# A graph layer with a guarded fast path: the guard taken from bounds ahead of the last tiles, and its branch placed in front of the last two scatters

## The chip, the cores and the metric

The kernel runs on one core of a Trainium2 chip. The time is device time in microseconds (us), the median of several executions. One further execution was recorded by the hardware profiler; its span runs from the first to the last instruction of the program.

## The reference

One layer of a graph transformer on 3125 nodes with 256 features each, and 53125 weighted edges sorted by their target. It adds three things to its input `x`:

```python
xn = _layernorm(x)
x = x + gnn(xn, edges) + mix(xn)          # graph convolutions; linear attention
x = x + ffn(_layernorm(x))                # mixture of 8 experts, one per token
# inside ffn
pos = (cumsum(one_hot, axis=0) * one_hot).sum(-1) - 1
kept = pos < C                            # C = 489 slots for each expert
hmid = relu(einsum('ecd,edf->ecf', buf, w1) + b1[:, None, :])     # 256 -> 1024
ybuf = einsum('ecf,efd->ecd', hmid, w2) + b2[:, None, :]          # 1024 -> 256
y = nan_to_num(ybuf[idx, min(pos, C - 1)] * (prb * kept)[:, None], posinf=1e4, neginf=-1e4)
```

The graph part multiplies sparse sums of edges (`segment_sum`) with two small weights, each followed by a softmax. `nan_to_num` is what the guard of this case is about: where every expert's output is finite, it changes nothing.

## The kernel before

**Two versions of one layer.** `network(runs)` is traced twice. `network(True)` relies on things that the inputs may or may not satisfy: edges sorted by target so that every group of five nodes has its edges in one run of 128 (`from_runs`), certain counts of tokens for each expert, and finite outputs, so that `nan_to_num` can be left out. While it runs it gathers a verdict: `held["found"]` (all edges were found), `full` and `low` (the counts), and `row_sums`, one sum for each token and tile of the experts' outputs (`OUTER` = 24 tiles). At its end all are multiplied into one number, `right`. Then every engine loads `right` into a register and meets a branch: with `right` = 0 the whole layer is computed again by `network(False)`, which makes no assumption; otherwise it is jumped over.

**Stages of `network(True)`.** First, `from_runs` builds the dense 3125 x 3125 adjacency matrix in 40 batches of 16 groups (`batch`, L627: matmuls of two selection matrices, copied by ACT, written to DRAM by two DMAs of the SP queue, L649 and L650). Beside that, rows of it are read back (`load_rows`, L652, tiles `a` in the pool `first_a`): strip 0 in tiles tagged `a0`, and the first rows of strip 1 in tiles tagged `a1`, some of them asked for ahead of the last batches (L715). All of this stage has a hand-written order on every engine (`tc.manual_schedule()`), and the queue of SP takes writes and reads in that order. The tiles are consumed in the order in which they were asked for (`take`, L675). Then three passes of dense products over all strips follow (L272, tiles `at`), with the attention and the gating beside them.

**The experts.** Tokens are scattered into `xbuf`, with slots for each expert. The experts' slots are worked through in halves of up to 256 slots. For each half: `turned` (L1113) normalizes the rows (DVE, tile `xs` in the pool `normed`, two buffers), transposes them on TensorE and copies them with ACT; `inner` (L1132) makes 8 blocks of hidden units with Relu on ACT; `outer` (L1148) multiplies them with w2, in tiles of 128 slots, adds the weighted bias (`bx`, L1162) and the residual (`y`, L1174, both DVE, from the pool `fin`), and scatters the rows into `out` with an indirect DMA of POOL (L1192). `chain` interleaves the halves: transposes of a half, then the second matmuls of the half before, then its own first matmuls. `outer` is a generator that yields after half of a tile's matmuls and between tiles. In this stage TensorE's order is written by hand; the order of the other engines is found by a planner, which simulates the program and puts an instruction where its engine would otherwise be idle.

**The end.** The last half has 233 slots, one tile of 128 and one of 105. Behind its last `y` stand the check of the row sums (L1521, L1522), a matmul that adds up over the partitions (L1527), `right_i` (L1529), the register loads (L1537), the branch (L1538) and the program's closing instructions (L1585). On the path that jumps over `network(False)`, each engine raises its semaphores by what the skipped code would have raised; POOL does it for the queues of its own DMAs with one instruction (INC_SWDGE_SEM), after waiting until they have landed.

Of the kernel before, what the change touches and what calls it, by code (L numbers as in the profile page):

```python
# [62 lines left out]

EPS = 1e-5
FMAX = 3.4028234663852886e38


def rows_all(ap, offset, n):
# [5 lines left out]
def gps_layer(ctx: ExitStack, tc: tile.TileContext, a: dict, out: bass.AP):  # L74
# [202 lines left out]
    def load_constants():  # L277
# [61 lines left out]

        return finish()  # L340

    def network(runs):

        with ExitStack() as net:
            layer(net, runs)

    def layer(net, runs):
# [67 lines left out]
        def from_runs():  # L415
# [136 lines left out]
            pre = ph.enter_context(tc.tile_pool(name="pre", bufs=2))  # L552
            wide = ph.enter_context(tc.tile_pool(name="wide", bufs=2))
            stage = ph.enter_context(tc.tile_pool(name="stage", bufs=3))
            first_a = ph.enter_context(tc.tile_pool(name="first_a", bufs=4))
            ps_0 = [acc(0) for _ in range(2)]
            some, made = {}, {}
            last = NG // GB
# [91 lines left out]
                nc.sync.dma_start(rows[112:GP], st[112:GP, :ng, :])  # L650

            def load_rows(s, c, tag):  # L652
                at = first_a.tile([P, SW], FP, tag=tag, name=tag)
                k = P if c < NT - 1 else LAST
                c0 = STRIPS[s][0] * P
                nc.sync.dma_start(at[:k], adj_rows[c * P : c * P + k, c0 : c0 + SW])
                return at
# [22 lines left out]
            for b in range(last + 1):  # L680
                c = (min(NG, (b + 5) * GB) - 1) // GC
                turned = c not in turned_c
                s, step = (b - NORM_AT) // NORM, (b - NORM_AT) % NORM
                normed = 0 <= s < len(STRIPS)
                if turned:
                    turn_ends(c, *fetched[c])
                if normed and step == 0:
                    norm_a(s)
                if normed and step == 1:
                    norm_b(s)  # L690
                if normed and step == 3:
                    norm_c(s)
                if b in (22, 23):
                    next(finish, None)
                if b == 24:
                    load_w_kv()
                if b < last:
                    prepare(b + 1)
                batch(b)
                if normed and step == 3:  # L700
                    norm_d(s)
                if turned:
                    q, _ = fetched[c]
                    turn_some(c, q, edge_h, 1, 2)
                    turn_some(c, q, edge, 0, 3)
                    count(c, q)
                    if c > 1 and c + 2 < NC:
                        fetched.append(gather(c + 2))
                if b in (4, 6):
                    search(1 + b // 2)  # L710
                if b == 4:
                    fetched.append(gather(3))
                while (todo[0][1] + 1) * P <= (b - 1) * GB * GR:
                    ask()
                if last - 6 < b <= last - 2:  # L715
                    ask(more, ready_1, "a1")
                while len(ready) > 2 and b > NORM_AT + 1:
                    take()
# [293 lines left out]
        net.callback(mm_pools.remove, mm_pools[-1])  # L1012
        wts_0 = net.enter_context(tc.tile_pool(name="wts_0", bufs=EARLY, side="right"))
        xe_0 = net.enter_context(tc.tile_pool(name="xe_0", bufs=EARLY, side="right"))
        fin = net.enter_context(tc.tile_pool(name="fin", bufs=4, side="right"))
        hm_0 = net.enter_context(tc.tile_pool(name="hm_0", bufs=EARLY, side="right"))
        xeT_0 = net.enter_context(tc.tile_pool(name="xeT_0", bufs=1, side="right"))
        normed = net.enter_context(tc.tile_pool(name="normed", bufs=2, side="right"))
# [38 lines left out]
        def early_experts():  # L1057
# [42 lines left out]
                    early[r] = [early[r], xe, HALF, space_0]  # L1100
            return early, num, row, full, low

        if runs:
            tiles_done = iter(range(OUTER))
            row_sums = ranked.tile([P, OUTER], FP, name="row_sums")
            nc.vector.memset(row_sums, 0.0)
        else:
            lim = ranked.tile([P, 3], FP, name="lim")
            nc.vector.memset(lim[:, 0:1], 1e4)
            nc.vector.memset(lim[:, 1:2], -1e4)  # L1110
            nc.vector.memset(lim[:, 2:3], 0.0)
# [18 lines left out]
            nc.scalar.copy(xeT[:, :, :slots], pt.rearrange("p (d s) -> p d s", d=2)[:, :, :slots])  # L1130

        def inner(xeT, hm, w1, b1_e, slots):  # L1132
            for f in range(FC):
                p = acc(f)
                for d in range(2):
                    nc.tensor.matmul(  # L1136
                        p[:, :slots], w1[:, d, f * P : (f + 1) * P], xeT[:, d, :slots],
                        start=(d == 0), stop=(d == 1),
                    )
                nc.scalar.activation(  # L1140
                    hm[:, f, :slots], p[:, :slots], AF.Relu, bias=b1_e[:, f : f + 1], scale=1.0
                )

        def apart(group, ins):
            tc.declare_no_dep(ins.ins, group=group, reason="tokens have rows of their own")
            tc.add_to_no_dep_group(group, ins.ins)

        def outer(hm, xe, w2, b2_e, slots, group):  # L1148

            for j, c in enumerate(range(0, slots, P)):  # L1150
                n = min(P, slots - c)
                p = mm()
                for f in range(FC):
# [4 lines left out]
                    if f == FC // 2 - 1:  # L1158
# [7 lines left out]
                            if group == "early":  # L1166
                                tc.keep_in_program_order(weighted_bias)
                        yield
                y = fin.tile([P, D], FP, tag="y", name="y")[:n]
                if runs:  # L1170


                    k = next(tiles_done)
                    nc.vector.scalar_tensor_tensor(  # L1174
                        y, p[:n, :D], xe[:n, j, D + 2 : D + 3], bx, op0=ALU.mult, op1=ALU.add,
                        accum_out=row_sums[:n, k : k + 1],
                    )
                else:

                    nc.vector.tensor_tensor(y, p[:n, :D], b2_e[:n], ALU.add)  # L1180
                    nc.scalar.activation(y, y, AF.Copy, scale=xe[:n, j, D + 2 : D + 3])
                    for i in range(3):
                        mk = masks.tile([P, D], I32, tag="mk", name="mk")[:n]
                        if i == 0:
                            nc.vector.tensor_scalar(mk, y, FMAX, None, op0=ALU.is_gt)
                        elif i == 1:
                            nc.vector.tensor_scalar(mk, y, -FMAX, None, op0=ALU.is_lt)
                        else:
                            nc.vector.tensor_tensor(mk, y, y, ALU.not_equal)
                        nc.vector.copy_predicated(y, mk, lim[:n, i : i + 1].to_broadcast([n, D]))  # L1190
                    nc.vector.tensor_tensor(y, y, xe[:n, j, :D], ALU.add)
                sc = nc.gpsimd.indirect_dma_start(  # L1192
                    out=out,
                    out_offset=bass.IndirectOffsetOnAxis(
                        ap=xe[:n, j, D + 3 : D + 4].bitcast(I32), axis=0
                    ),
                    in_=y,
                    in_offset=None,
                    bounds_check=N - 1,
                    oob_is_err=False,  # L1200
                )
                apart(group, sc)
                if c + P < slots:
                    yield

# [6 lines left out]
        def chain(group, halves):  # L1212

            for (w1, w2, b1_e, b2_e), xe, slots, space in halves:
                xeT, hm = space()
                turned(xe, slots, xeT, group == "early")
                yield
                if front:
                    yield from outer(*front.pop())
                inner(xeT, hm, w1, b1_e, slots)  # L1220
                front.append((hm, xe, w2, b2_e, slots, group))
                yield

        def space_0():
# [160 lines left out]
        with tc.manual_schedule(engines={mybir.EngineType.PE}):  # L1385
# [115 lines left out]
            def work():  # L1501
                for i, (r, skip, n) in enumerate(todo):
# [5 lines left out]
                    for q, skip_q, _ in todo[i : i + 2 if runs else i + 1]:  # L1508
                        if q not in have:
                            have[q] = weights(q)  # L1510
                    yield have[r], rows_of.pop(i), n, space

            with tc.issue_after(gate_ins.ins):
                for _ in chain("out", work()):
                    pass
                outer_end(*front.pop())
            if runs:

                finite = ranked.tile([P, OUTER], FP, name="finite")
                n_finite = ranked.tile([P, 1], FP, name="n_finite")  # L1520
                nc.vector.tensor_scalar(finite, row_sums, -FMAX, None, op0=ALU.is_ge)  # L1521
                nc.vector.scalar_tensor_tensor(  # L1522
                    finite, row_sums, FMAX, finite, op0=ALU.is_le, op1=ALU.mult,
                    accum_out=n_finite,
                )
                total = mm()
                nc.tensor.matmul(total[:1, :1], ones[:, 0:1], n_finite, start=True, stop=True)  # L1527
                held["right"] = keep.tile([1, 1], I32, tag="right", name="right_i")
                nc.vector.scalar_tensor_tensor(  # L1529
                    held["right"], total[:1, :1], P * OUTER - 0.5, right, op0=ALU.is_ge,  # L1530
                    op1=ALU.mult,
                )

    network(True)


    right_v = nc.values_load(held["right"][0:1, 0:1], min_val=0, max_val=1)  # L1537
    with tc.If(right_v < 1, preferred_fallthrough_block=False):  # L1538
        network(False)


# [47 lines left out]
```

## Time and profile before

| | |
|---|---|
| median of 3 executions | 1028.1 us (1026.73 to 1030.35) |
| profiled execution | 1029.22 us |
| its span | 1027.6 us |
| granted clock of TensorE, mean over the span | 0.981 |
| busy: TensorE, DVE, ACT, POOL | 984.9, 514.0, 296.9, 92.0 us |

Engines are called PE (TensorE, matmuls), PEld (its weight loads), DVE (VectorE), ACT (ScalarE), POOL (GpSimd) and SP (SyncE, which here only issues DMAs); a `q` behind a name stands for the engine's sequencer, which waits, branches and issues. L1192 is line 1192 of the kernel. A row of instructions gives the engine, the operation, what it writes and reads, how many there were, their time, and in brackets the idle time before with what ended it. In the list of one source line the three durations are the shortest, the median and the longest in nanoseconds, and the two times behind are those of the first and the last start. In the chain of waits each row is start, length, and who held the chain. In the table by stretch the columns are the stretch, its length, then busy time and instructions of PE, PEld, DVE, ACT and POOL, the granted clock, the share of the DMA engines and GB/s.

### The profile page before, as it was taken

The numbers are of one execution on the slowest core, as the hardware profiler recorded it, in microseconds if no ns is written. First come the engines' busy times: TensorE is split into PE (matmuls) and PEld (weight loads), VectorE is DVE, ScalarE is ACT, GpSimd is POOL, SyncE is SP. The second block draws the span as 40 slices with busy tenths as digits, with TensorE's granted clock in tenths as the row PEclk, the third lists the DMA queues.
The fourth block names the chain that finished last, engine by engine and source line by source line (L and its number), as shares of the span: only waits on it lengthen the run. The fifth ranks groups of instructions, "written<-read, shape, count | busy, mean of one in ns | idle before, by whom it ended". The sixth has DMA issues, their size and how long they took to land.

```text
span 1027.6 us, 11418 instructions
## 1 busy us (share of the span) xinstructions
PE 984.9 (96%) x4198; PEld 642.5 (63%) x4198; DVE 514.0 (50%) x1144; ACT 296.9 (29%) x541; POOL 92.0 (9%) x103
## 2 busy tenths in 40 slices
PE   4999999979999999999999999999999989999995
PEld 3878888854444444455675554474444568898884
DVE  7989799800234434444653675584344454322110
ACT  2879989830001000101101001110111214222231
POOL 6301000000000000000000000000021232111111
PEclk8999999989999999999999999999999999999998
DMA  4979888983844237521375658669899886613300
GB/s 121 271 207 255 247 238 234 257 240 107 274 151 151 97 103 220 150 72 55 97 258 199 212 198 274 222 201 376 309 299 299 259 287 227 226 40 118 122 18 15
DMA packets 173104, 197.95 MB, mean 193 GB/s; under 512 B 8758, under 2 KB 119894, under 8 KB 173037
## 3 DMA queue, kind: packets, MB, share of 16 engines
q1 hardware_dynamic: 165997, 179.02, 55.8%
q0 software_dynamic: 6912, 18.10, 5.7%
q8 instruction: 35, 0.57, 0.2%
q14 instruction: 32, 0.26, 0.1%
q10 hardware_dynamic: 128, 0.00, 0.0%
HBM read 144.43 MB, written 53.37 MB: 192 GB/s over the span
## 4 chain that ended last, share of the span: by engine, by line
PE 82%; DVE 4%; DMA 3%; ACT 2%; issue 1%; SPq 1%; POOL 0%; POOLq 0%; ACTq 0%; DVEq 0%
PE acc L272 48%; PE mm L1154 7%; PE acc L1136 6%; PE acc L636 5%; PE b L636 5%; PE mm L813 4%; PE mm L869 2%; DMA at<-adj 2%; PE pk L841 1%; PE mm L896 1%; PE mm L993 1%; ACT rhs L621 1%; DMA xbuf<-rows,s_idx 1%; ACT st_rows L640 1%; PE mm L1255 0%
## 5 line engine op out<-in xcount | busy, mean ns | idle before, releaser
L272 PE MATMUL acc<-at,xn 128*128 128x512 f32 (+3 forms) x540 | 203.2, 523 | 0.9 <-DMA at<-adj 0.9
L272 PEld LDWEIGHTS acc<-at,xn 128*128 128x128 f32 (+1 forms) x540 | 96.5, 190 | 88.9 <-issue 75.3
L272 PE MATMUL acc<-at,late 128*128 128x512 f32 (+4 forms) x350 | 139.3, 549 | 3.2 <-DMA at<-adj 3.2
L272 PE MATMUL acc<-at,g 128*128 128x512 f32 (+4 forms) x350 | 137.8, 541 | 0.0
L272 PEld LDWEIGHTS acc<-at,late 128*128 128x128 f32 (+1 forms) x350 | 64.1, 195 | 63.1 <-issue 54.3
L272 PEld LDWEIGHTS acc<-at,g 128*128 128x128 f32 (+1 forms) x350 | 62.9, 190 | 58.6 <-issue 52.3
L636 PE MATMUL acc<-rhs,lhs 128*125 128x128 f32 x626 | 87.5, 284 | 8.4 <-ACT rhs L621 5.5
L636 PEld LDWEIGHTS acc<-rhs,lhs 128*125 128x125 f32 x626 | 79.3, 195 | 19.4 <-issue 7.9
L608 DVE TENSOR_TENSOR lhs<-in_row,in_blk 128x1000 f32<-128x1000 f32 (+1 forms) x79 | 90.2, 1183 | 1.6 <-DVE in_row L585 0.5
L636 PE MATMUL b<-rhs,lhs 128*125 128x128 f32 x624 | 83.4, 278 | 0.0
L272 PE MATMUL acc<-a,xn 128*128 128x512 f32 (+1 forms) x160 | 76.4, 620 | 5.2 <-DMA a<-adj 5.2
L636 PEld LDWEIGHTS b<-rhs,lhs 128*125 128x125 f32 x624 | 77.0, 194 | 0.0
L621 ACT CAST rhs<-cells 128x2048 f32<-128x2048 bf16 x39 | 74.8, 1919 | 1.2 <-DVE cells L599 1.2
L826 ACT ACTIVATE sq<-kv 128x512 f32<-128x512 f32 x25 | 15.7, 630 | 179.3 <-DVE kv L822 179.3
L1154 PE MATMUL mm<-w,hm 128*128 128x256 f32 (+2 forms) x288 | 64.3, 380 | 0.0
L819 DVE TENSOR_REDUCE kmean<-mm 128x8 f32<-128x512 f32 x25 | 17.3, 691 | 91.6 <-PE mm L813 91.6
L1136 PE MATMUL acc<-xeT,w 128*128 128x208 f32 (+2 forms) x288 | 58.1, 360 | 0.7 <-ACT xeT L1130 0.7
L1154 PEld LDWEIGHTS mm<-w,hm 128*128 128x128 f32 (+2 forms) x288 | 51.2, 180 | 9.6
L1136 PEld LDWEIGHTS acc<-xeT,w 128*128 128x128 f32 x288 | 53.3, 190 | 4.4 <-ACT xeT L1130 0.9
L640 ACT COPY st_rows<-acc 125x512 f32<-125x512 f32 (+1 forms) x79 | 47.7, 604 | 23.7 <-issue 15.1
L272 PEld LDWEIGHTS acc<-a,xn 128*128 128x128 f32 (+1 forms) x160 | 29.9, 199 | 36.7 <-issue 29.5
L1140 ACT ACTIVATE hm<-acc,b_e 128x256 f32<-128x256 f32 (+2 forms) x72 | 32.6, 455 | 69.0 <-PE acc L1136 68.9
(242 smaller groups left out, 1039.0 us busy)
## 6 DMA issues: line engine op xcount, KB each, us to landing
at<-adj SPq DMA_DIRECT2D x52, 1280.0 KB
adj<-st_rows SPq DMA_DIRECT2D x39, 896.0 KB
at<-adj SPq DMA_DIRECT2D x14, 1024.0 KB
at<-adj SPq DMA_DIRECT2D x12, 960.0 KB
w<-in_f_w SPq DMA_DIRECT2D x10, 1024.0 KB
a<-adj SPq DMA_DIRECT2D x39, 256.0 KB
at<-adj SPq DMA_DIRECT2D x12, 452.5 KB
adj<-st_rows SPq DMA_DIRECT2D x39, 104.0 KB
```

The source lines that it names most:

```text
L272: nc.tensor.matmul(ps[d][:, :w], stationary(c, d)[:k], a_rows[:k, :w], start=(c == 0), stop=(c == NT - 1),)
L608: nc.vector.tensor_tensor(lhs[:, j::k], in_row[:, j::k, :, None].to_broadcast([P, m, GR, CA]), in_blk[:, :, None, :, j].to_broadcast([P, m ...
L621: nc.scalar.copy(rhs.rearrange("p (i j) c -> p i j c", j=2), cells.rearrange("p i c j -> p i j c"),)
L636: nc.tensor.matmul(p[:GP, j * P : (j + 1) * P], lhs[:, j0 + j], rhs[:, j0 + j], start=True, stop=True,)
L640: nc.scalar.copy(st[:GP, j0 : j0 + nj, :], p[:GP, : nj * P].rearrange("p (g b) -> p g b", b=P),)
L813: nc.tensor.matmul(pkv, xnT[:, d, t * P : (t + 1) * P], w_kv[:, d, :], start=(d == 0), stop=(d == 1),)
L819: nc.vector.tensor_reduce(mean, p3, AX.X, ALU.add)
L826: nc.scalar.activation(sq, kv, AF.Square, scale=0.125)
L869: nc.tensor.matmul(p[:, j * D : (j + 1) * D], xnT[:, d, (t0 + j) * P : (t0 + j + 1) * P], w_mix[:, d, :], start=(d == 0), stop=(d == 1),)
L1136: nc.tensor.matmul(p[:, :slots], w1[:, d, f * P : (f + 1) * P], xeT[:, d, :slots], start=(d == 0), stop=(d == 1),)
L1140: nc.scalar.activation(hm[:, f, :slots], p[:, :slots], AF.Relu, bias=b1_e[:, f : f + 1], scale=1.0)
L1154: nc.tensor.matmul(p[:n, :D], hm[:, f, c : c + n], w2[:, f, :], start=(f == 0), stop=(f == FC - 1),)
```

## The change

The verdict is made earlier, from bounds instead of the last outputs:

- For the last half, Relu on ACT also gives the sums of the hidden units (`accum_out`, 8 columns of `bounds`), and five new Square activations (`squares`) give the sums of squares of this expert's w2 and b2 (5 columns). If all of these are at most 1e15, the last two tiles can't overflow. The outputs of the squares are thrown away; their tiles are taken from the buffers of `xs`.
- After half of the last half's first tile, DVE checks the 22 row sums so far and the 13 bounds, two small matmuls add them up, and DVE makes `right` and `right_i`. The register loads (`load_right`) stand ahead of the last `y`.
- After the first tile, a further matmul (`each`) spreads `right` over the partitions; DVE adds `FAR` to the tokens of the last two tiles where `right` is 0, so that their scatters fall outside of `out` and are dropped.
- The last half's outputs go into a tile of their own (`y_end`), and its two scatters are issued after the branch and after the jumped-over code. POOL and DVE have a hand-written order in this last stretch.
- For the room, `first_a` has three buffers for `a1` instead of four, with one load fewer ahead of the last batches, and `fin` has three buffers instead of four.

```diff
-            first_a = ph.enter_context(tc.tile_pool(name="first_a", bufs=4))
+            first_a = ph.enter_context(tc.tile_pool(name="first_a", bufs=1))
...
-                at = first_a.tile([P, SW], FP, tag=tag, name=tag)
+                at = first_a.tile([P, SW], FP, tag=tag, name=tag, bufs=4 if tag == "a0" else 3)
...
-                if last - 6 < b <= last - 2:
+                if last - 5 < b <= last - 2:
                     ask(more, ready_1, "a1")
...
-        fin = net.enter_context(tc.tile_pool(name="fin", bufs=4, side="right"))
+        fin = net.enter_context(tc.tile_pool(name="fin", bufs=3, side="right"))
...
         def inner(xeT, hm, w1, b1_e, slots):
+            sums = {}
             for f in range(FC):
+                if final:
+                    sums = {"accum_out": bounds[:, f : f + 1]}
...
                 nc.scalar.activation(
-                    hm[:, f, :slots], p[:, :slots], AF.Relu, bias=b1_e[:, f : f + 1], scale=1.0
+                    hm[:, f, :slots], p[:, :slots], AF.Relu, bias=b1_e[:, f : f + 1], scale=1.0,
+                    **sums,
+                )
+
+        def squares(w2, b2_e):
+            for i in range(FC // 2 + 1):
+                of = w2[:, 2 * i : 2 * i + 2, :] if i < FC // 2 else b2_e
+                junk = normed.tile([P, 2, D], FP, tag="xs", name="squares")
+                nc.scalar.activation(
+                    junk if i < FC // 2 else junk[:, 0, :], of, AF.Square,
+                    accum_out=bounds[:, FC + i : FC + i + 1],
                 )
...
+                if ends and c + P >= slots:
+                    final["load"]()
+                y = y_end[:n, j, :] if ends else fin.tile([P, D], FP, tag="y", name="y")[:n]
+                if ends:
+                    nc.vector.scalar_tensor_tensor(
+                        y, p[:n, :D], xe[:n, j, D + 2 : D + 3], bx, op0=ALU.mult, op1=ALU.add
+                    )
+                elif runs:
...
+                if not ends:
+                    apart(group, to_rows(y, xe[:n, j, D + 3 : D + 4].bitcast(I32)))
...
+                    if i == len(todo) - 1 and runs:
+                        squares(have[r][1], have[r][3])
+                        final.update(load=load_right, xe=rows_of[i])
                     yield have[r], rows_of.pop(i), n, space
...
-                outer_end(*front.pop())
...
+                ending = outer(*front.pop())
+                final_tiles = P, CAP - HALF - P
+                if runs:
+                    next(ending)
+                    n_sums = OUTER - 2
...
+                    n_bounds = bounds.shape[1]
+                    nc.vector.scalar_tensor_tensor(
+                        finite[:, :n_bounds], bounds, BOUND, ones[:, :n_bounds], op0=ALU.is_le,
+                        op1=ALU.mult, accum_out=n_finite[:, 1:2],
+                    )
+                    total = mm()
+                    for i in range(2):
+                        nc.tensor.matmul(
+                            total[:1, :1], ones[:, 0:1], n_finite[:, i : i + 1], start=(i == 0),
+                            stop=(i == 1),
+                        )
...
+                    nc.vector.tensor_copy(right_i, right)
+                with tc.manual_schedule(engines={mybir.EngineType.Pool, mybir.EngineType.DVE}):
+                    if runs:
+                        next(ending)
+                        each = mm()
+                        nc.tensor.matmul(each[:, :1], ones[0:1, :], right, start=True, stop=True)
+                        far = ranked.tile([P, 1], FP, name="far")
+                        nc.vector.tensor_scalar(
+                            far, each[:, :1], 0.5, float(FAR), op0=ALU.is_lt, op1=ALU.mult
+                        )
...
+                    for _ in ending:
+                        pass
...
-    right_v = nc.values_load(held["right"][0:1, 0:1], min_val=0, max_val=1)
-    with tc.If(right_v < 1, preferred_fallthrough_block=False):
+    with tc.If(held["right"] < 1, preferred_fallthrough_block=False):
         network(False)
+    for scatter in held["ends"]:
+        scatter()
```

## The prediction

> **What bounds the kernel now.** I read the page first (engine shares, then the chain that ended last).
>
> ```profile
> PE 984.9 (96%) x4198; PEld 642.5 (63%) x4198; DVE 514.0 (50%) x1144; ACT 296.9 (29%) x541; POOL 92.0 (9%) x103
> PE 82%; DVE 4%; DMA 3%; ACT 2%; issue 1%; SPq 1%; POOL 0%; POOLq 0%; ACTq 0%; DVEq 0%
> ```
>
> TensorE is the chain nearly everywhere, so work on DVE, ACT or POOL costs nothing unless it makes PE wait or lies behind the last matmul. Next, the chain of waits over the last stretch, and the instructions of L1538 (the branch) and L1585 (the program's end).
>
> ```profile
> 1008.07 6.92 PE mm L1154 x32
> 1014.99 0.03 issue
> 1015.01 0.50 DVE y L1174 x2
> ...
> 1015.80 0.99 POOL out L1192
> ```
> ```profile
> L1538 POOLq EVENT_SEMAPHORE  x5: 17/43/43, 1016.9 to 1017.2; - x5
> L1538 POOLq COMPARE_BRANCH  x2: 41/44/48, 1016.8 to 1019.5; - x2
> ...
> L1538 POOLq INC_SWDGE_SEM  x1: 1192/1192/1192, 1018.3 to 1018.3; - x1
> ```
> ```profile
> L1585 POOLq EVENT_SEMAPHORE  x4: 17/17/17, 1026.8 to 1027.5; - x4
> L1585 POOLq DRAIN  x3: 46/109/4219, 1022.5 to 1027.3; - x3
> ```
>
> The chain stops at the last scatter, yet the span ends at 1027.6, 12.6 us after the last matmul. Those 12.6 us are POOL's queue: y and the check until the register loads at 1016.4 (L1537); comparison and waits, 0.8; the increment (1.19), which starts only at 1018.3, when the last scatter (issued 1015.8, median landing 2.5) has landed; the jump at 1019.5, whose target starts at 1022.5, so 3.0; a drain of 4.2; closing semaphores, 0.8. The others jump earlier and are ready earlier: ACT drains at 1019.6, DVE 1020.4, PE 1021.3, SP 1023.4. POOL sets the end.
>
> A second place matters, because the diff takes one early load away. The chain of waits from 200 on, and the busy time by stretch:
>
> ```profile
> 217.81 1.03 SPq L656
> ...
> 219.36 2.79 SPq L650
> ...
> 222.25 4.00 DMA a<-adj
> ...
> 226.29 33.27 PE acc L272 x72
> ```
> ```profile
> 215.00:220.00 5.00, 2.27 (x10) 1.12 (x8) 0.00 (x0) 0.94 (x3) 0.00 (x0) 0.99 0.99 289
> 220.00:225.00 5.00, 3.78 (x4) 1.18 (x4) 0.00 (x0) 0.00 (x0) 0.00 (x0) 0.50 0.98 282
> 225.00:230.00 5.00, 3.71 (x5) 1.65 (x6) 0.18 (x1) 0.00 (x0) 0.00 (x0) 0.50 0.47 146
> ```
>
> PE waits 3.7 and 1.6 us for the rows `a`, while the DMA engines are 98 to 99% busy: there bytes set the time. The last three columns are TensorE's granted clock, the DMA share and GB/s: after the wait the clock is 0.50.
>
> **The change, part by part.** The sum is made on the profiled execution, 1029.22 us with a span of 1027.6, so 1.6 lie around it; the median of the runs is 1028.1, 1.1 lower, and I carry the difference over to it.
>
> *The tail.* The check now needs the last half's relu sums, the squares and 22 row sums. PE's part of it stands after half of the first tile: 1008.07 + 6.92/4 = 1009.8. The last relu starts at 1008.10 (0.46), its accumulator read takes 0.19 (L1270's row), the DVE check of the bounds 0.3 (L1522: 0.18 + 0.08): ready at 1009.1 to 1009.4. From that matmul to the loads it was 1016.0 to 1016.4; with a second matmul (0.16) and one more DVE copy (0.14, as L1529) 0.7: loads at 1010.5. POOL has nothing in flight then (its last scatter before the branch was issued at 1002.58), so its queue runs 0.8 + 1.2 + 3.0 without a wait: at the jump's target at 1015.6. There the two scatters stand, 1.28 apart (L1360's spacing) and 0.98 long, 2.3 together. The second y is ready at 1015.5 plus what PE got: three small matmuls now stand inside its work, at most 0.19 each (L1527, both records), 0.3 to 0.6; with 0.4 y is there at 1015.9, hidden for the second scatter. If both have to wait for DVE's count after its branch, they start at 1016.0. They end at 1017.9 to 1018.3; I take 1018.1. The drain, 4.2: 1022.3; closing 0.8: 1023.1 against 1027.6, **−4.5**; I take −4.4, for a register move or two. What is late next: PE's jump, 3.9 us (L1538), from about 1016 ends at 1020; SP's closing waits took 2.6 (1020.8 to 1023.4) and, with the second scatter landed at 1017.1 + 2.5 = 1019.6, end by 1022.2. Both stay just inside the drain.
>
> *The new waits.* On PE, `total` waits for DVE's check, with one and a half tiles queued behind it: ready 1009.4, reached 1009.8, so 0, and 0.4 us of margin. `each` waits for DVE's `right` (1010.4) and is reached after the first tile, at 1011.5: 0. On DVE `far`, two index additions (0.2 each, as the small L1521) and a register load (0.55, L1537) stand ahead of the last y, in the 3 us in which DVE idles now (1012.0 to 1015.0): 0. On POOL the load waits for `right_i`; behind it only the branch and the two scatters are queued. The first scatter goes 3.3 us later than now (1012.33), and only the end waits for it.
>
> *ACT's squares.* Four of 128x512 and one of half that, 0.63 (L826) + 0.19 each: 3.9 us. w2 of this expert was loaded long before. Their outputs take turns in the two `xs` buffers, and the last half's xs comes after them, so its norm (now at 968.32, needed at PE's transposes at 994.4) waits for the fourth. ACT's timeline has the place:
>
> ```profile
> 981.96 0.51 ACT L1130 COPY xeT<-mm 128x416 f32<-128x416 f32 x1
> 989.88 0.81 ACT L1140 ACTIVATE hm<-acc,b_e 128x208 f32<-128x208 f32 x2 [7.42 <-PE acc L1136]
> ```
>
> 7.4 us idle, from when the buffer is free (transposes at 981.9): done by 986.4, norm by 987, 7 us early. Cost 0, covered by that idle time; the third rival prices its loss. A table load isn't in the sum: after the one at L136 Relu, Copy, Exp and Tanh run without one, and Square ran beside Sqrt; Square after Exp is not shown. Two loads at L136's 1.28 make 6.5 us, still inside 7.4: 0. The Trainium skill (ScalarE: Activation LUTs, What ACT_TABLE_LOAD costs) gives about 2.66 us per switch with its drain; by an estimate from that page, 3.9 + 5.3 = 9.2 us would overrun the gap by 1.8. The relu reads add 0.19 to 0.46 in a period of 0.79: 0.
>
> *One early load fewer.* A tile of 128 x 512 floats is 262 KB; at 285 GB/s (rows above) 0.9 us. The rows PE waits for land up to 0.9 earlier; half of that is lost, since the clock is 0.50 until 230 and PE fills the time at half speed. Afterwards five tiles of lead (1.72 each, 8.6 us) stand against landings of 4.0, so no new wait. From 0 to −0.9; I take **−0.5**, the bytes' row at half clock. DMA is only 50% busy later, so the shifted load is free.
>
> *Fewer `fin` buffers.* Three y buffers at 3.5 us a tile are 10 us, against 0.8 + 2.5 until a scatter has landed: 0. y and bx of the last half: one accumulator read less each, 0.08, hidden. Buffers decide when the planner lets bx run ahead, so DVE's order may shift in the experts' stage; PE is busy there 10.0 of every 10 us from 960 to 1010, and DVE at most 2.0: 0.
>
> Sum: −4.4 − 0.5 = −4.9: span 1022.7, profiled 1024.3, median **1023.2**.
>
> **The rivals.**
> 1. *The drain starts its work when the last scatter has landed.* The trace shows it only with nothing in flight. Second scatter at 1017.1 + 2.5 = 1019.6, + 4.2 + 0.8 = 1024.6: −3.0, with the load −3.5: 1024.6. For it: a drain has something to wait for now. Against: 4.2 us of it ran 4.2 us after everything had landed, so it isn't mainly a wait.
> 2. *No gain: the end stays tied.* Either the drain ends a fixed time after the last scatter (1015.8 to 1026.7, 10.9 us; 1017.1 + 10.9 + 0.8 = 1028.8, +1.2), or the change doesn't do what it says, and POOL's branch is held until the last y (1016.0 + 0.8 + 1.2 + 3.0 + 2.3 + 4.2 + 0.8 = 1028.3, +0.7). With the load 1028.3 to 1028.8. Against the first: POOL does nothing recorded from 1019.5 to 1022.5; against the second: in the present trace each engine branches 0.4 to 0.8 after its own load, without a common wait.
> 3. *Slower: the squares stand behind the previous half's relus.* Place: ACT after 994.9. Four squares, 3.3, end at 998.2, the norm at 999.1; the transposes, which stand ahead of a whole half's matmuls in PE's fixed order, start 4.7 late. After such a wait (3.7 above) the clock was 0.50 for 10 us; over the 6.9 us of the next matmuls that loses about 3.4. +8.1 − 4.9 = +3.2: 1031.3. It decides once the fourth square ends after 993.6, a norm ahead of 994.4. Against it: DVE's order is not the program's; the last half's bx ran at 989.38, ahead of y at 998.36, which is written before it, so the planner fills idle time:
>
> ```profile
> 989.38 0.48 DVE L1162 SCALAR_TENSOR_TENSOR bx<-b_e,xe 105x256 f32<-105x256 f32 x1
> ...
> 998.36 0.48 DVE L1174 SCALAR_TENSOR_TENSOR y<-mm,xe,bx 128x256 f32<-128x256 f32 x1 [8.49 <-PE mm L1154]
> ```
>
> The Trainium skill (TensorE: Matmul & The Clock Gate, What's actually happening) lets the array return after some 3.4 us of work, an estimated 1.7 lost instead of 3.4 and a net of about +1.5; the row, with a second wait inside, shows 10 us.
>
> **How the numbers follow.** Forecast 0.52, rival 1 0.14, rival 2 0.19, rival 3 0.15. About 0.3% (3.1 us) can be told from no change in this kernel. Faster by more: the forecast and most of rival 1, 0.64; within: 0.22, rival 2 and the rest of rival 1; slower: 0.14. Low end: the load at −0.9, scatters not waiting for DVE (−0.2) and 1.0 for the drain, whose size the trace has only once: 1021.6; high end takes in rival 2: 1029.0. What is left out is rival 3 and a little below.
>
> **What would show it.** Right: POOL's jump near 1012.5, scatters at 1015.6 to 1016 and 1.3 later, a drain of 4.2 beginning near 1018, span near 1022.7; squares on ACT between 968 and 989 and PE unbroken from 960 on; the wait for `a` near 217 about 0.9 shorter. Wrong: a drain of 5 us or more (rivals 1, 2), PE idle ahead of L1126 (rival 3), POOL's branch after the last y.

## The result, and the profile after

| | before | after |
|---|---|---|
| median of the runs compared | 1028.4 us (6 runs, 1026.7 to 1030.4) | 1023.4 us (6 runs, 1020.5 to 1025.4) |
| ratio, 95% interval | | 0.9950 (0.9931 to 0.9968) |
| profiled execution, its span | 1029.2, 1027.6 us | 1024.3, 1022.7 us |

Faster by 5.1 us (0.5%), of which the interval allows 3.3 to 7.1. The prediction was 1023.2, with a span of 1022.7. That the span agrees to the tenth is partly luck, as the experiments show.

The page of the changed kernel, its engine shares and its chain that ended last:

```profile
span 1022.7 us, 11450 instructions
...
PE 983.0 (96%) x4202; PEld 640.3 (63%) x4202; DVE 514.4 (50%) x1148; ACT 300.6 (29%) x559; POOL 89.4 (9%) x103
...
POOLq 0%; POOL 0%; issue 0%
POOLq L1664 0%; POOL out L1169 0%
```

PE still works 96% of the span. The chain that ended last is now 2.3 us long (1015.33 to 1017.65) and lies wholly on POOL: it breaks off just ahead of the first of the two scatters, and no matmul is part of it any more. The rows of the branch (L1615), the register load (L1546) and the program's end (L1664), and POOL's timeline:

```profile
L1615 POOLq EVENT_SEMAPHORE  x5: 17/43/43, 1009.7 to 1010.1; - x5
L1615 POOLq COMPARE_BRANCH  x2: 41/44/48, 1009.6 to 1011.3; - x2
...
L1615 PEldq COMPARE_BRANCH  x2: 95/1862/3630, 1011.6 to 1014.9; - x2
...
L1615 POOLq INC_SWDGE_SEM  x1: 1152/1152/1152, 1010.1 to 1010.1; - x1
```
```profile
L1546 POOLq TENSOR_LOAD <-right_i x1: 297/297/297, 1009.3 to 1009.3; - x1
```
```profile
L1664 POOLq EVENT_SEMAPHORE  x4: 17/17/17, 1021.9 to 1022.6; - x4
L1664 POOLq DRAIN  x3: 46/115/6066, 1015.8 to 1022.4; - x3
```
```profile
1015.39 0.98 POOL L1169 DMA_INDIRECT out<-y_end,to_end  x1 [12.98 <-DVEq L1615]
1016.68 0.98 POOL L1169 DMA_INDIRECT out<-y_end,to_end  x1 [0.30 <-issue]
```

Read them as one queue. The load is at 1009.3 (1016.4 before). The increment begins at 1010.1, right behind the waits: no scatter is in flight that it would have to wait for, where before it started 1.0 us after the last wait, at 1018.27, just behind the landing of the last scatter that the trace records at 1018.25. The jump is issued at 1011.3 and its target starts at 1013.9. The scatters are at 1015.39 and 1016.68, 1.28 apart. The long drain is recorded from 1015.8, while the scatters still run; it ends at 1021.8, 4.17 after the second scatter's end (1017.66). The increment, the jump and its landing place are now all done while PE still multiplies; before, they came after it. DVE's timeline has the work that had to be ready:

```profile
1007.59 0.17 DVE L1570 SCALAR_TENSOR_TENSOR finite<-bounds,ones 128x13 f32<-128x13 f32 x1 [5.88 <-ACT hm L1150]
...
1009.09 0.14 DVE L1585 CAST right_i<-right 1x1 int32<-1x1 f32 x1
...
1014.77 0.48 DVE L1204 SCALAR_TENSOR_TENSOR y_end<-mm,xe,bx 105x256 f32<-105x256 f32 x1 [2.63 <-PE mm L1185]
```

The verdict stands 5.7 us ahead of the last y; before it came after it.

Absolute times of two profiles can't be subtracted here: at the last half's relus PE is 1.09 us earlier than in the profile before, for reasons that turn out not to be the change's. So I count from the start of the last Relu (1007.01 in the changed kernel, 1008.10 before), and call the time from there to the end of the span the tail. e1, e2 and e12 are experiments that follow below:

| us after the last Relu's start | predicted | after | before | scatters ahead (e1) | late verdict (e2) | two steps earlier (e12) |
|---|---|---|---|---|---|---|
| POOL's register load | 2.4 | 2.25 | 8.30 | 8.29 | 7.65 | 1.39 |
| jump issued | 4.4 | 4.31 | 11.39 | 12.48 | 9.71 | 3.44 |
| its target starts | 7.5 | 6.90 | 14.40 | 15.27 | 12.58 | 6.05 |
| first end scatter | 7.5 to 7.9 | 8.38 | 4.22 | 4.90 | 14.05 | 7.53 |
| last y starts | 7.3 | 7.76 | 6.91 | 7.76 | 6.91 | 7.77 |
| second scatter's end | 10.0 | 10.64 | 8.69 | 9.52 | 16.31 | 9.79 |
| long drain's end | 14.2 | 14.81 | 18.62 | 19.48 | 20.48 | 13.96 |
| end of the span | 15.0 | 15.66 | 19.47 | 20.34 | 21.34 | 14.83 |

The tail is shorter by 19.47 − 15.66 = 3.8 us. A second profile of the changed kernel gives 15.69. Part of the 3.8 is the jump, which took 3.0 us in the one profile of before. In e3, whose program ends as the kernel before does, the jump took 2.66 and the tail 19.11, so the gain can also be read as 3.4 to 3.5 us:

```profile
L1538 POOLq COMPARE_BRANCH  x2: 41/44/48, 1016.3 to 1019.0; - x2
...
L1585 POOLq DRAIN  x3: 46/109/4218, 1021.6 to 1026.4; - x3
```

### The profile page after: what moved, and what is told of

Its sections match the earlier page's. It is cut to its first block, busy times and chain, and to the rows that moved or that the text cites. A ratio compares the mean times of both kernels' runs of the same rounds, so it can differ in the third digit from the quotient of the medians.

```text
span 1022.7 us, 11450 instructions
## 1 busy us (share of the span) xinstructions
PE 983.0 (96%) x4202; PEld 640.3 (63%) x4202; DVE 514.4 (50%) x1148; ACT 300.6 (29%) x559; POOL 89.4 (9%) x103
## 3 DMA queue, kind: packets, MB, share of 16 engines
q0 software_dynamic: 6912, 18.10, 5.8%
```

## The experiments

Theory O: the gain needs the early verdict and the scatters behind the branch together, since the increment ahead of POOL's jump waits for a scatter's landing. Its rivals gave the gain to one of the two alone, or to the removed load.

**e1: the scatters ahead of the branch again, the early verdict kept.**

```diff
+    for scatter in held["ends"]:
+        scatter()
     with tc.If(held["right"] < 1, preferred_fallthrough_block=False):
         network(False)
-    for scatter in held["ends"]:
-        scatter()
```

> The changed kernel with its two last scatters put back ahead of the branch; verdict, squares, buffers and the early load stay as changed. Theory O (the gain is POOL's landing wait, increment and jump, hidden beside the last tiles because the scatters stand behind the branch): POOL's increment has to wait for the last landing again, so from the start of the last y to the end 12.6 us as in the kernel before (changed kernel: 7.9); with 0.85 us more on PE and 0.5 less for the load the time is 1028 to 1029.5 us, no gain. Rival V (the early verdict alone pays, since check and register loads leave the path): that part is 1.4 us shorter, 11.2 us from the last y to the end, and about 1027 us.

Measured: 1028.3 against 1029.4 (ratio 0.9997, 0.9984 to 1.0010). The rows of the scatters, of POOL's increment and of the drain in e1:

```profile
1011.17 1.09 POOL L1169 DMA_INDIRECT out<-y_end,to_end  x1 [9.50 <-DVE to_end L1597]
1014.82 0.98 POOL L1169 DMA_INDIRECT out<-y_end,to_end  x1 [2.56 <-DVEq L1617]
```
```profile
L1617 POOLq COMPARE_BRANCH  x2: 41/44/48, 1014.9 to 1018.7; - x2
L1617 POOLq INC_SWDGE_SEM  x1: 1192/1192/1192, 1017.5 to 1017.5; - x1
```
```profile
L1664 POOLq DRAIN  x3: 46/109/4218, 1021.5 to 1026.3; - x3
```

The verdict was known at 1008.5, more than 5 us before the last y, and SP and ACT loaded it at once. It was worth nothing to POOL: its own load came only at 1014.6, with the wait for the last y in front of it on the queue, and the increment sits at 1017.53, 2.7 after the second scatter's start (2.5 in the profile before) and 0.03 after that scatter's landing, which the trace records at 1017.50. Jump and drain follow it. The run doesn't separate these two delays; both come of scatters queued ahead of the branch. The tail is 20.34, longer than before by 0.87, which is the 0.85 by which the small matmuls delay the last y. The rival that gave the early verdict a share of its own falls.

**e2: the scatters behind the branch, the verdict after the last y.** The bounds and the squares stay; count, small matmuls and loads move behind the last y.

```diff
+                    for _ in ending:          # both tiles first
+                        pass
                 ... check of the sums and bounds, total, right_i, each, far, to_end ...
+                    load_right()
```

> The changed kernel with the verdict's matmuls and register loads put behind the last tile; the scatters stay behind the branch. Theory O: the increment has no landing to wait for, but the chain runs after the last y: verdict 0.65, comparison and waits 0.8, increment 1.15, jump 2.6 to 3.0, waits 0.7, scatters 2.3, drain 4.2, closing 0.85: 13.2 to 13.6 us from the last y to the end, some 5.5 more than the changed kernel, time 1028 to 1029.5 us. Rival S (the order of scatters and branch alone pays, because nothing waits for a landing): 11.5 us or less from the last y, 1026.5 us or less.

Measured: 1030.6 against 1029.4 (ratio 1.0015, 1.0005 to 1.0025). POOL's increment and scatters in e2:

```profile
L1612 POOLq INC_SWDGE_SEM  x1: 1152/1152/1152, 1016.6 to 1016.6; - x1
```
```profile
1022.12 0.98 POOL L1169 DMA_INDIRECT out<-y_end,to_end  x1 [18.66 <-issue]
1023.41 0.98 POOL L1169 DMA_INDIRECT out<-y_end,to_end  x1 [0.30 <-issue]
```

The increment no longer waits for a landing (it follows the last wait at once), but the scatters now come after increment and jump: tail 21.34, 1.87 longer than before, and 0.8 to 1.2 more than expected. That miss has the place of the one in the prediction: from the jump's target (1020.65) to the first scatter it takes 1.47 us, although the last of the other engines' jumps, PE's, has ended by 1020.9 and the last y long before. Eight waits take 0.7 of it, and 0.54 pass between the last wait and the next register move, in which the profile shows nothing that POOL waits for. The changed kernel has the same 1.47 (1013.92 to 1015.39). Order alone loses, the early verdict alone gains nothing: Theory O stands.

**e3: the removed early load alone, on the kernel before** (the `first_a` lines of the diff and nothing else).

> The kernel before with only the early load taken away (three a1 buffers, one load fewer ahead of the last batches). Prediction's step: PE reaches the end of the matmuls on a 0.5 us earlier (between 0 and 0.9), counted from the last batch; the time is 1027.9 us if that stays, 0.05%, which the timing can't tell from none. Rival G (it is given back at the next wait for at rows, as the one profile of the changed kernel suggests: 0.5 gained near 220 and 1.0 lost near 268): the shift is gone or reversed behind that wait, time 1028.4 to 1029.

Measured: 1029.1 against 1029.4 (ratio 1.0000, 0.9989 to 1.0011): at most about 1.1 us either way. In its trace PE's lead over the profile before shrinks from 1.86 to 1.15 us between 200 and 280, a loss of 0.7. All thirteen profiles with this edit can be read so: what PE loses (plus) or gains (minus) between 200 and 280 against the profile before runs from −3.1 to +1.8 us, with a mean of −0.1. In the changed kernel's own two profiles it is +0.5 and −2.7. Nor is the wait for the rows `a` about 0.9 shorter, as the prediction said: PE sat idle for them for 5.2 us before, and for 5.3 in e3, 5.1 and 4.5 in the two profiles of the changed kernel. A term of −0.5 can't be seen in that, and all of it leans on a single profile of before.

**e4: the two end scatters left out** (the last 128 and 105 tokens of the last expert are not written).

> The changed kernel without its last two scatters (the rows of the last half's tokens aren't written). POOL then meets its drain at the jump's target with nothing in flight. Theory F (the drain is a fixed piece of work of 4.2 us from its issue): it ends at about 3.4 us after the start of the last y, PE's jump (3.6 us, ending 3.9 after the last y) becomes the last one, and the end is 4.8 us after the start of the last y, span 3.1 us under the changed kernel's. Rival W (the drain is mostly a wait for scatters to land and retire): it is under 2 us here.

Measured: one run, 1022.7, span 1021.0. From the last Relu to the end 12.24 instead of 15.66, so 3.4 less. The span shows only 1.7 because PE was 1.8 us later than in the changed kernel when it reached the last half. Rows of the end in e4:

```profile
L1662 POOLq DRAIN  x3: 46/109/4056, 1015.6 to 1020.7; - x3
...
L1662 DVEq DRAIN  x2: 10/34/58, 1020.1 to 1020.5; - x2
L1662 PEldq DRAIN  x2: 8/8/8, 1020.2 to 1020.5; - x2
```

POOL's drain ends at 1019.7 and then waits for DVE and PE, whose jumps end at 1020.1 and 1020.2. So PE's jump is what comes next once POOL is out of the way, some 3.4 us below POOL's end. The drain took 4.06 us with no scatter in flight, so it isn't mainly a wait for scatters, and rival W falls.

**What sets the first scatter?** In the changed kernel DVE raises its count (its semaphore, by what the jumped-over code would have raised) after its branch at 1015.30, and the scatter starts at 1015.39; by POOL's row it waited for DVE. If so, PE's small matmuls cost time (theory D). If POOL's own queue needs 6.1 us from the load, they don't (theory Q).

**e5: the broadcast folded into the first group of small matmuls.**

```diff
+                    nc.tensor.matmul(total[:, :1], ones[0:1, :], right, start=True, stop=False)
                     for i in range(2):
                         nc.tensor.matmul(
-                            total[:1, :1], ones[:, 0:1], n_finite[:, i : i + 1], start=(i == 0),
+                            total[:, :1], ones, n_finite[:, i : i + 1], start=False,
...
-                        each = mm()
-                        nc.tensor.matmul(each[:, :1], ones[0:1, :], right, start=True, stop=True)
```

> The broadcast of the old verdict is folded into the first group of small matmuls (three in one group, answer on all 128 partitions), the second group and one DVE copy go. PE should then be about 0.4 us late at the last y instead of 0.85, and the register load perhaps 0.15 earlier. Theory D (both end scatters wait for DVE's count, raised after the last y, so PE's 0.85 is on the path): last y to the end of the span stays 7.9, so the end comes 0.45 earlier after the start of the last half. Theory Q (POOL's own queue, 6.1 us from its register load to the first scatter, sets the end; PE's time is hidden by 0.1 us): the end moves with the load only, 0.1 to 0.2 earlier, and last y to the end grows to about 8.2.

Measured: one run, 1025.1, span 1023.4. Both expectations of the edit itself were wrong. PE's timeline in e5:

```profile
1007.53 0.38 PE L1575 MATMUL mm<-right,ones 1*128 1x1 f32 x2
1007.84 0.61 PE L1577 MATMUL mm<-n_finite,ones 128*128 128x1 f32 x4
```

The group takes 0.9 us; in the changed kernel the four of `total`, with a weight tile of one column, took 0.24. The last y starts 7.86 after the last Relu, so PE lost 0.95 instead of 0.85, and the load came 0.5 later (2.75). Still the scatter answers the question: it starts 0.75 after DVE's count, by POOL's queue alone.

**e11: the same kernel again**, because its drain had ended 5.3 after the second scatter's end.

> The folded kernel once more. In its first run the second scatter took 4.2 us from its start until SP saw it landed, and POOL's drain ended 5.3 us after the scatter's end; in every other profile these were 2.5 and 4.2. If that was chance, 2.5 and 4.2 are back; if it comes with the kernel, 4.2 and 5.3 again. The register load should again be 0.5 later against PE than in the changed kernel, since the six passes of the folded group take 0.95 us where four took 0.28.

Measured: one run, 1027.9; 4.17 from the scatter's end to the drain's end, and 2.96 from the second scatter's start to the end of SP's wait for it. So the 5.3 doesn't come with the kernel. The load is again 0.5 later (2.75). The tail is 16.43, 0.8 longer than the changed kernel's: 0.5 from the load, and the rest from a jump of 2.87 us instead of 2.59.

**e7: the first group of small matmuls one step earlier** in the first of the two last tiles.

```diff
-                    if f == FC // 2 - 1:
+                    if f == FC // 2 - (2 if ends else 1):
```

> The first group of small matmuls stands one step (two of PE's 0.21 us matmuls, 0.43 us) earlier in the first of the last two tiles; nothing else is changed, PE still late by 0.85 at the last y. Theory Q (POOL's queue from the register load sets the first scatter): load and first scatter 0.43 earlier against the last y, last y to the end 7.5 instead of 7.9. Theory D (DVE's count sets it): last y to the end stays 7.9, the first scatter 0.1 after DVE's count, and load to first scatter grows from 6.1 to 6.5.

Measured: one run, 1020.0, span 1018.3. PE reached the last Relu 4.0 us earlier than in the changed kernel's profile, ahead of anything that the edit touches, so the time says nothing here; the tail is 15.25, shorter than the changed kernel's by 0.41. Its DVE and POOL timelines, and DVE's count:

```profile
1010.82 0.48 DVE L1204 SCALAR_TENSOR_TENSOR y_end<-mm,xe,bx 105x256 f32<-105x256 f32 x1 [2.63 <-PE mm L1185]
```
```profile
1011.02 0.98 POOL L1169 DMA_INDIRECT out<-y_end,to_end  x1 [12.56 <-issue]
1012.30 0.98 POOL L1169 DMA_INDIRECT out<-y_end,to_end  x1 [0.30 <-issue]
```
```profile
L1615 DVEq EVENT_SEMAPHORE  x1: 21/21/21, 1011.3 to 1011.3; - x1
```

The first scatter starts at 1011.02, while the last y is still being computed (1010.82 to 1011.30) and 0.3 before DVE raises its count. It does not wait for DVE's count; theory D falls, and the releaser that the profile names in the changed kernel (`<-DVEq L1615`) is merely the event nearest in time. POOL's queue, 6.1 us from load to scatter (6.12, 6.14, 6.14 in the changed kernel, its repeat and e7; 6.38 and 6.40 in e5 and e11, whose jumps took 2.9), sets the end.

**e8: both edits; e9: the changed kernel once more.**

> Both edits of the two runs before, the version meant to beat the changed kernel. PE late by 0.4 instead of 0.85 at the last y and the load 0.4 to 0.6 earlier. Theory D: end 0.45 earlier than the changed kernel's, counted from the start of the last half; theory Q: 0.4 to 0.6 earlier. Either way about 0.05% of the time, which five rounds can hardly show (1022.9 if the changed kernel has 1023.4); the trace shows it.

> The changed kernel once more, as it is. Ratio to before 0.993 to 0.997 again. In its profile the tail must stay: last y to the end of the span 7.9 (12.6 before), PE 0.85 late in the last two tiles. If the 1.6 us by which PE was ahead of the earlier profile from 60 us on belongs to the change, it is there again; if it is the phase of the clock's dips, it has another size. The half microsecond of the removed load: gained by 260 and given back by 280 if the giving back belongs to the change; another balance, anywhere within some 2 us, if it is chance.

Measured: e8 1023.1 (ratio 0.9951, 0.9937 to 0.9964), e9 1023.5 (0.9960, 0.9947 to 0.9973), before 1027.9. e8's tail is 15.74, no gain: the fold gives back what the step earns. e9 repeats the tail (15.69), the last y 7.76 after the Relu, and PE's lead of 1.65 us from 65 on. That lead is no part of the change: e3, whose one edit takes effect after 200, shows 1.86, while e4 and e12, which hold all of the change up to there, show 0.0 and 0.1. The stretch 60 to 65 in before and in after says why; the columns are those of the table by stretch:

```profile
60.00:65.00 5.00, 5.00 (x33) 5.00 (x34) 4.93 (x7) 4.25 (x7) 0.00 (x0) 0.71 0.75 211
```
```profile
60.00:65.00 5.00, 5.00 (x36) 4.07 (x35) 4.93 (x7) 4.85 (x8) 0.00 (x0) 1.00 0.68 193
```

The granted clock was 0.71 before and 1.00 after, at the same work. In e4 and e12, without a lead, it was 0.71 and 0.66 in this stretch; in e3 and e9, with one, 1.00.

**e12: two steps earlier** (`FC // 2 - 3`), the best version that the experiments point to.

> The first group of small matmuls two steps (0.86 us) earlier than in the changed kernel, at the point where the count of the bounds is just ready, so PE may wait for it by 0.2. Load and first scatter 0.7 to 0.86 earlier against the start of the last half, the end as much: last y to the end 6.9 to 7.2 instead of 7.9. The median would be 0.7 to 0.9 below the changed kernel's, less than five rounds resolve (ratio about 0.9945 where the changed kernel has 0.9955); if the wait on PE costs more than its hiding place, the gain is smaller.

Measured: 1023.9 against 1029.3 (ratio 0.9945, 0.9924 to 0.9965). Tail 14.83, 0.83 shorter than the changed kernel; last y to end 7.06 instead of 7.90; PE no later than with the changed kernel (7.77). The trace shows the gain, the intervals of the times don't separate the two. POOL's queue still sets the end.

**e6: forty more small DMAs on POOL; e10: a long transfer behind the last scatter.** Two questions on the drain.

```diff
+            for i in range(40):                                   # e6, mid-kernel
+                nc.gpsimd.dma_start(extra[16 * i : 16 * i + 16, :], ident[:16, :])
...
+    nc.gpsimd.dma_start(extra, adj[0 : P * 2048].rearrange(...))  # e10, behind the end scatters
```

> The changed kernel with 40 more small DMAs (8 KB each, into a scratch tensor) issued on POOL in the middle of the kernel, long landed by the end. If POOL's drain at the end works off something for each DMA that POOL has issued (81 in the changed kernel in 4.2 us, some 0.05 each), it takes about 2.1 more: from the second scatter's end to the drain's end 6.2 instead of 4.17, and the increment ahead of the jump about 1.7 instead of 1.15. If both are fixed, 4.17 and 1.15 stay.

> The changed kernel with one more DMA on POOL behind the two end scatters, a copy of 1 MB in DRAM into a scratch tensor, whose landing takes 5 us or more instead of the scatter's 2.5. Theory fixed: the drain ends 4.2 us after POOL's last issue, whatever is in flight (and SP, which waits for the landing, ends after it). Theory landing: the drain ends 2.1 to 2.7 us after the last landing (2.07 in the first run of the folded kernel, whose scatter landed late, 2.67 in the changed kernel), so some 3 to 6 us later than the fixed theory has it. Rival 1 of the prediction (landing plus a whole 4.2) would be 1.5 to 2 us later still.

Measured: one run each, 1028.9 and 1028.3; the question is the drain, not these times. Increment, drain and queue of e6, then the drain and the last DMA of e10:

```profile
L1619 POOLq INC_SWDGE_SEM  x1: 1332/1332/1332, 1013.1 to 1013.1; - x1
```
```profile
L1668 POOLq DRAIN  x3: 115/184/6807, 1019.1 to 1026.8; - x3
```
```profile
q0 software_dynamic: 8192, 18.43, 6.1%
```
```profile
L1666 POOLq DRAIN  x3: 46/115/10136, 1015.5 to 1026.3; - x3
```
```profile
1017.00 0.59 POOL L1620 DMA_DIRECT2D extra<-adj  x1
```

In e6 the drain ends 4.90 after the second scatter's end instead of 4.17, and the increment takes 0.18 more. POOL's queue had 8192 packets instead of 6912: 4.90/8192 and 4.17/6912 are both 0.60 ns a packet, and before (4.22 for 6912) and e4 (4.06 for 6816) give 0.61 and 0.60. The 4.17 came back in every one of the seven profiles that have 6912 packets, both scatters behind the branch and no late landing (4.16 to 4.17), so the 4.90 of the single run e6 stands clear of it. So the drain grows with what POOL has issued over the whole kernel, and by these two nearly in proportion to packets. It does not go by the number of DMAs: 40 added 0.73, while the two scatters that e4 leaves out account for 0.16. In e10 the last issue ends at 1017.59 and SP sees the transfer landed at 1023.5; the drain ends at 1025.7, 8.1 after the issue and 2.1 after the landing. With e5's first run (2.07 after its late landing) the rows fit one rule: with the changed kernel's packets, the drain ends 4.17 after the end of POOL's last issue or 2.1 after the last landing, whichever is later. In the changed kernel the landing (1019.15) is 2.7 before the drain's end and does not count.

## Why the prediction was right, and where it was not

**The mechanism** held, step by step: the load right after the bounds, an increment without a wait, the jump behind PE's work, then the scatters and the drain. e1 and e2 show that neither half of the change gains alone.

**The tail** was put at −4.4 and measured −3.8 (−3.4 to −3.5 against e3). The mis-sized terms, by the table: the load 0.15 earlier than expected; the jump 2.6 instead of 3.0 (2.5 to 3.0 over all profiles, the 3.0 being the one shown before); and, missing from the sum, the 1.47 us from the jump's target to the first scatter, for which the text allowed "a register move or two". e2 shows that they are POOL's own. The prediction's other reason for a later scatter, a wait for DVE's count, gave about the right place (1016.0 for 1016.5 on the same clock) for a reason that e7 refutes.

**PE's three small matmuls** took 0.85, not 0.4: from start to start they hold PE for 0.17 and 0.31, and about 0.09 more is lost ahead of each of the two groups and again behind it. The step "hidden for the second scatter" still held, with more to hide (times after the Relu's start): y is ready at 8.24, and the second scatter starts at 9.66.

**The early load**, −0.5, is not shown. e3 bounds it to about 1.1 us either way. In the profile after, PE gains half a microsecond between 200 and 260 and has lost 1.0 again by 280; in the repeat it gains 2.7 by 280. Since the wait for `a` hardly changed in the profile after, even the half there doesn't come about as predicted; what makes these differences stays open.

So the span of 1022.7 came out by compensation: the tail gave 0.6 less than forecast, and PE, 1.1 us ahead (1.6 ahead from the dip of the clock, less 0.5 lost at the loads), gave 0.6 more than the load's term. The difference of the medians over the two comparisons of the changed kernel, −5.1 and −4.4, agrees with a tail of −3.8 within the intervals.

**The squares** cost nothing, as forecast, but earlier than thought. ACT's timeline after:

```profile
967.28 0.55 ACT L1137 COPY xeT<-mm 128x466 f32<-128x466 f32 x1
967.72 0.63 ACT L1159 ACTIVATE squares<-w 128x512 f32<-128x512 f32 x1
...
971.06 0.19 ACT L1159 ACTIVATION_READ_ACCUMULATOR squares<-b_e 128x1 f32 x1
```

They ran from 967.7 to 971.3, one behind the other, and did not wait for the transposes (981.9 before) at which the prediction had the buffers come free. Its own row of the norm, at 968.32 before, shows that a buffer was free by then. In the profile after, the last half's norm follows the last square at 971.28, and the transposes need it at 993.2, 22 us later:

```profile
971.28 0.41 DVE L1124 TENSOR_SCALAR xs<-xe 128x256 f32<-128x256 f32 x1
```

No table load stands among the squares, so the figure of the Trainium skill (ScalarE: Activation LUTs, What ACT_TABLE_LOAD costs) was not called upon here. PE was busy 10.0 of every 10 us from 960 to 1010.

**The rivals.** Rival 1 (the drain starts its work at the landing) is out for this kernel: the drain ended 2.7 after the landing, not 4.2. But its argument against was too strong: e10 shows that a drain does wait for a landing, with 2.1 behind it. Rival 2: the drain ended 5.1 after the second scatter's start instead of 10.9, and POOL's branch did not wait for the last y. Rival 3 needed squares behind the previous half's relus; they stood 26 us ahead of the last of them.

## What to carry to other kernels

After the last matmul, look for the one engine whose queue still has the longest list, and count everything on it: waits, increments, jumps, register moves and the drain. Moving a branch ahead of the last work paid here only because nothing that it waits for, the landing of a scatter, was left in flight ahead of it, and because its verdict came early enough to hide the jump. Compare two profiles by stretches that start at a common event, not by their ends, and doubt a named releaser whose event is only near in time: move one of the two and look again.

## What the runs showed of the hardware

- POOL's drain at the end took 4.06, 4.17, 4.22 and 4.90 us for 6816, 6912, 6912 and 8192 packets that its queue had moved in the whole kernel. (In the 4.17 and the 4.90 the time counts from the end of the last scatter, which ran after the drain was issued; the other two are the drain's own length.) A kernel whose end hangs on POOL might thus gain from moving early plain transfers to other queues; that wasn't tried. Whether packets or something near them is counted stays open: the slope is 0.57 ns a packet between after and e6, but 1.7 between e4 and before.
- The same drain ended 2.1 us after a landing that came late (e10, and e5's first run).
- POOL's increment began 0.02 to 0.03 us after the landing of the last scatter issued ahead of it (before, e1, e3), and at once where that scatter had long landed (after, e2).
- From the issue of a jump over the skipped code to its target POOL needed 2.5 to 3.0 us, and from the target to the first scatter there 1.47 us, in which the profile shows no other engine to wait for.
- PE's position at 200 us differed by up to 2.2 us between profiles with the same work, depending on where a dip of the granted clock (0.71 in the stretch from 60 to 65) fell.
